# A cross-attention and RWKV-style layer in float32: the recurrence's four feature chunks are taken two at a time instead of one at a time

## The chip, the cores and the metric

The program runs on one core of one Trainium2 chip. The metric is the device time of one execution in microseconds (us). Four executions of the kernel before gave a median of 1838.74 us (1835.77 to 1843.25).

## The reference

The batch has 32 sequences of 128 tokens with 512 features, all in float32. Layer 0 is a cross attention over features, layer 1 an RWKV-style block whose core is a linear recurrence over the tokens.

```python
# layer 0, per sequence b (128 x 512)
A  = softmax((Wn @ inorm(x) + bn).T @ (Wm @ inorm(ctx) + bm))
x  = Wo @ ((Wl @ ctx + bl) @ A.T) + bo + x
# layer 1 (H = 32 heads of S = 16; its state comes from ctx)
xa = ln(x); sx = shift(xa)
xk, xw, xv, xr, xg = xa + sx * (maa + lowrank(xa + sx * maa_x))
w  = exp(-exp(time_decay + tanh(xw @ td_w1) @ td_w2))
r, k, v = xr @ Wr.T, xk @ Wk.T, xv @ Wv.T;  g = silu(xg @ Wg.T)
def step(s, r_t, k_t, v_t, w_t):              # per head, s is 16 x 16
    a   = outer(k_t, v_t)
    out = r_t @ (u * a + s)
    return a + w_t[:, None] * s, out
x1  = x + groupnorm(out) * g @ Wo.T
xc  = ln(x1); sx2 = shift(xc)
out = x1 + sigmoid((xc + sx2 * mr) @ Wfr.T) * (square(relu((xc + sx2 * mk) @ Wfk.T)) @ Wfv.T)
```

## The kernel before

**Tiling.** The 32 sequences are cut into `NG` = 8 groups of `G` = 4. A group's activations stand with features on the partitions: four feature chunks `c` of 128 features (8 heads) by `N` = 4 x 128 = 512 token columns. For each group the kernel runs `layer0` on its four sequences (stage "first"), and `layer1`: a "front" (norm, token shift, the five mixed inputs, the gates), the "recurrence" for each of the four chunks, and a "back" (group norm, the product with Wo, the feed-forward).

**The order is made by a planner.** No instruction is issued where the code names it. Every call goes to a recorder `K` (line 229 is where all recorded operations are emitted, so that nearly all the profile's rows say L229), and `schedule` then lists the operations of all engines in an order of its own: at each step it takes the operation that can start soonest by a table of costs, among equals the one with the lower rank, which is the place in the code less a little for what hangs on it. `with K.bunch(ns)` makes several matmuls one indivisible operation. Tiles come from pools with fixed numbers of slots: 54 work tiles `t` of 128 x 512, 8 PSUM `bank`s, two `rk`, two of each of the four `at`, two `vp`. An operation cannot be placed until its tile has a slot.

**The recurrence of one chunk** (`recurrence`, line 831) is a doubling scheme over the tokens. `r` and `k` lie side by side in one tile `rk`, `v` in a work tile; each comes from four accumulated matmuls (`proj`) and a ScalarE copy. Distances 1 and 2 are done by elementwise products on VectorE and a matmul with the block matrix `sum_bc` (banks `d0`, `d1`, `d2`). Then come four levels `l` = 4, 8, 16, 32, each of which is a handoff chain:

1. ScalarE makes `r2`, the right halves of `r` with even and odd heads masked apart (two `ACTIVATE t<-rk,par`).
2. TensorE multiplies `k` and `r2` in a bunch of 32 small matmuls on 32 x 64 tiles of the array into four banks `pa` (the bunch named 843 in the code).
3. VectorE copies the valid blocks from `pa` into the four `at` tiles (`COPY_PREDICATED`; at the last level ScalarE copies).
4. `twice(l)` multiplies the half blocks of `rk` in place by the running decays (`TENSOR_TENSOR rk<-rk,...`), which the next level reads.

After the levels `k` is transposed (`pk`, copied to `kt`), a bunch `ps` of 16 matmuls forms the state at the middle of the sequence, VectorE makes `s1` of it, and TensorE forms the outputs in two banks `po`: one bunch of 32 matmuls with the state, and two of 32 with `vp` and `at`. VectorE adds `po` to `acc`.

A matmul in float32 shows as two passes in the trace, so that a bunch of 32 matmuls is a line "x64". The array is used in different tile shapes: 128*128 for the large products, 32*64 for `pa`, 64*32 for `ps` and the `at` bunches, 32*32 for the `po` bunch with the state.

**What stands around it.** `layer1` calls `decays` for two chunks together and then `recurrence` for each chunk, and after each chunk records `layer0` for one sequence of the next group, which gives the planner other work to put between the handoffs. The feed-forward of the last but one group is recorded after the last group's recurrence.

Of the kernel before, what the change touches and what calls it, by code (L numbers as in the profile page):

```python
# [13 lines left out]
AF = mybir.ActivationFunctionType  # L14
# [18 lines left out]
T_SLOTS, SMALL_SLOTS, W_SLOTS = 54, 40, 4  # L33
Q4 = 4
EPS = 1e-5

# [503 lines left out]
def xattn_then_rwkv(ctx: ExitStack, tc: tile.TileContext, a: dict, out: bass.AP):  # L540
# [11 lines left out]
    rks = Pool(slots("rk", 2, [P, 2 * N]))  # L552
    weights = Pool(slots("wring", W_SLOTS, [P, NC * E]))
    ats = [Pool(slots(f"at{q}_", 2, [P, G * 2 * C])) for q in range(Q4)]
    vps = Pool(slots("vp", 2, [P, G * Q4 * 2 * DM]))
# [8 lines left out]
    def wt(shape=(P, 512)):  # L564
        return View(Tensor(work, list(shape)))

# [207 lines left out]
    def norm_shift(xs, w, bname, row, g):  # L774
        xns = []
        for x in xs:
            stats = st_(1, 6)
            K.vector.bn_stats(stats[:, 0, :], x)
            mv, rstd = mean_rstd(stats, 1)
            xn = wt()  # L780
            K.vector.tensor_scalar(
                xn, x, mv[:, 0, 0:1], rstd[:, 0:1], ALU.subtract, ALU.mult
            )
            xns.append(xn)
# [29 lines left out]
    def decays(c, dlow):  # L814

        pe = [bank() for _ in range(2)]
        with K.bunch(1050):
            for i in range(2):
                half = slice(i * DD, (i + 1) * DD)
                K.tensor.matmul(  # L820
                    pe[i], td2[half, (c + i) * P : (c + i + 1) * P], dlow[half], start=True, stop=True
                )
        got = []
        for i in range(2):
            ex = wt()
            K.scalar.activation(ex, pe[i], AF.Exp, bias=v_("time_decay", c + i))
            K.scalar.activation(ex, ex, AF.Exp, scale=-1.0)
            got.append(ex)
        return got

    def recurrence(c, ex, xk, xr, xv, wk, wr, s0m):

        rk = View(Tensor(rks, [P, 2, N]))
        r, k = rk[:, 0], rk[:, 1]
        K.scalar.copy(r, proj(wr, xr, c))
        K.scalar.copy(k, proj(wk, xk, c))
        v = wt()
        K.scalar.copy(v, proj(wv, xv, c))
# [4 lines left out]
        vp = View(Tensor(vps, [P, G * Q4 * 2 * DM]))  # L843
        at = [View(Tensor(p, [P, G * 2, C])) for p in ats]
        pt = bank()
        for b in range(G):
            K.tensor.transpose(pt[:, b * P : (b + 1) * P], v[:, b * P : (b + 1) * P], ident)
        K.scalar.copy(
            vp.view(0, (2 * DM, G * Q4), (DM + S, 2), (1, S)),
            pt.rearrange("p (x y j) -> p x y j", x=G * Q4, y=2),  # L850
        )


        x0, x1 = wt(), wt()
        K.vector.scalar_tensor_tensor(x0, k, v_("u", c), r, ALU.mult, ALU.mult)
        K.vector.tensor_tensor(x1[:, 0 : N // 2], r[:, 1::2], k[:, 0::2], ALU.mult)
        sums = sum_bc.rearrange("p h s -> p (h s)")
        d0, d1 = bank(), bank()
        K.tensor.matmul(d0, sums, x0, start=True, stop=True)
        K.tensor.matmul(d1[:, 0 : N // 2], sums, x1[:, 0 : N // 2], start=True, stop=True)  # L860
        acc = wt()

        def twice(h, tot):


            nb = N // (2 * h)
            s = rk.view(h, (N - h, 2), (2 * h, nb), (1, h))
# [8 lines left out]
        x2 = wt()  # L876
        K.vector.tensor_tensor(
            x2.view(0, (4, nb), (2, 2), (1, 2)),
            rk.view(2, (4, nb), (1, 2), (0, 2)),
            rk.view(N, (4, nb), (0, 2), (1, 2)), ALU.mult,  # L880
        )
        d2 = bank()
        K.tensor.matmul(d2, sums, x2, start=True, stop=True)
        tot = twice(2, tot)

        for li, l in enumerate(LEVELS):

            r2 = wt([P, G * 2, C])
            nb = C // (2 * l)
            for x in range(2):  # L890
                K.scalar.activation(
                    r2.view(x * (C // 2), (C, G * 2), (l, nb), (1, l)),
                    rk.view(l, (C, G * 2), (2 * l, nb), (1, l)),
# [3 lines left out]
            with K.bunch(843):  # L897
                for b in range(G):
                    for n in range(2):
                        for q in range(Q4):  # L900
                            rows_q = slice(q * DM, (q + 1) * DM)
                            K.tensor.matmul(
                                pa[q][n * C : (n + 1) * C, b * C : (b + 1) * C],
                                rk[rows_q, 1, b * L + n * C : b * L + (n + 1) * C],
                                r2[rows_q, 2 * b + n],
                                start=True, stop=True,
                            )
            for q in range(Q4):
                if l < C // 2:
                    K.vector.copy_predicated(  # L910
                        at[q].view(l, (C, 2 * G), (2 * l, nb), (1, l)),
                        level[l].view(0, (0, 2 * G), (l, nb), (1, l)),
                        pa[q].view(0, (C // 2, 2 * G), (l, nb), (1, l)),
                    )
                else:
                    for n in range(2):
                        sl = slice(n * C, n * C + l)
                        K.scalar.copy(
                            at[q][sl, :, l : 2 * l],
                            pa[q][sl, 0 : N // 2].rearrange("p (x t) -> p x t", t=l),  # L920
                        )
            tot = twice(l, tot)
            if li == 0:
                t1, t2 = wt(), wt()
                K.vector.tensor_tensor(acc, d0, v, ALU.mult)
                K.vector.tensor_tensor(
                    t1[:, 0 : N // 2], d1[:, 0 : N // 2], v[:, 0::2], ALU.mult
                )
                K.vector.tensor_tensor(acc[:, 1::2], acc[:, 1::2], t1[:, 0 : N // 2], ALU.add)
                nb = N // 4  # L930
                K.vector.tensor_tensor(
                    t2.view(0, (4, nb), (2, 2), (1, 2)),
                    d2.view(0, (4, nb), (2, 2), (1, 2)),
                    v.view(0, (4, nb), (0, 2), (1, 2)), ALU.mult,
                )
                right = acc.view(2, (4, nb), (1, 2))
                for s in range(2):
                    K.vector.tensor_tensor(right, right, t2.view(s, (4, nb), (2, 2)), ALU.add)


        s0t = wt([P, G, 2 * S])
        K.vector.tensor_tensor(
            s0t, s0m.view(c * 2 * S, (NC * 2 * S, G), (1, 2 * S)), tot.view(0, (2, G), (0, 2 * S)),
            ALU.mult,
        )
        pk = bank()
        for b in range(G):
            K.tensor.transpose(pk[0:C, b * P : (b + 1) * P], k[:, b * L : b * L + C], ident)
        kt = wt([C, N])
        K.scalar.copy(kt, pk[0:C, :])  # L950
        ps = bank()
        with K.bunch(385):
            for b in range(G):
                for q in range(Q4):
                    K.tensor.matmul(
                        ps[q * DM : (q + 1) * DM, b * DM : (b + 1) * DM],
                        kt[:, b * P + q * DM : b * P + (q + 1) * DM],
                        vp[0:C].view((b * Q4 + q) * 2 * DM, (DM + S, 2), (1, S)),
                        start=True, stop=True,
                    )  # L960
        s1 = wt([P, G, 2 * S])
        for x in range(2):
            of_x = (x * S, (2 * S, G), (1, S))
# [7 lines left out]
        with K.bunch(1020):  # L971
            for b in range(G):
                for n in range(2):
                    for q in range(Q4):
                        sl = slice(q * DM, (q + 1) * DM)
                        i = (b * NC + c) * DM
                        K.tensor.matmul(
                            po[n][sl, b * C : (b + 1) * C],
                            s1[sl, b, :] if n else s0m[sl, i : i + DM],
                            r[sl, b * L + n * C : b * L + (n + 1) * C],  # L980
                            start=(b == 0), stop=False, skip_group_check=True,
                        )
        for half in range(2):
            with K.bunch(720):
                for b in range(half * G // 2, (half + 1) * G // 2):
                    for x in range(2):
                        for n in range(2):
                            for q in range(Q4):
                                sl = slice(n * C, (n + 1) * C)
                                i = (b * Q4 + q) * 2 * DM + x * DM  # L990
                                K.tensor.matmul(
                                    po[n][q * DM : (q + 1) * DM, b * C : (b + 1) * C],
                                    vp[sl, i : i + DM], at[q][sl, 2 * b + x, :],
                                    start=False, stop=(x == 1), skip_group_check=True,
                                )
        for n in range(2):
            o = acc.view(n * C, (L, G), (1, C))
            K.vector.tensor_tensor(
                o, po[n][:, 0 : G * C].rearrange("p (b t) -> p b t", b=G), o, ALU.add
            )  # L1000
# [3 lines left out]
    def layer1(g, xs):  # L1004
        following = []
        K.stage = ("front", g)
# [108 lines left out]
        for c in range(NC):  # L1115
            K.stage = ("recurrence", g, c)
            if c % 2 == 0:
                ex = decays(c, dlow)
# [3 lines left out]
            o.append(recurrence(c, ex[c % 2], xm["k"], xm["r"], xm["v"], wk, wr, s0m))  # L1122
            if g + 1 < NG:
                following.append(layer0((g + 1) * G + c))
# [137 lines left out]
```

## Time and profile before

| | |
|---|---|
| median of four executions | 1838.74 us |
| the profiled execution, its own time | 1839.27 us |
| its span in the profile | 1837.5 us |
| busy: TensorE (PE), VectorE (DVE), ScalarE (ACT), GpSimd (POOL) | 1794.7, 1227.6, 751.3, 309.6 us |
| instructions: PE, DVE, ACT | 20264, 2754, 1501 |
| mean granted clock of TensorE | 0.996 |

Busy time of an engine is the time in which at least one of its instructions runs; the matmuls' ends are modelled and overlap, so start-to-start differences in the timeline are what a matmul costs its engine. "<-X" beside an idle time names the engine whose work ended it. PEld is TensorE's weight load.

### The profile page before, as it was taken

Reading aid. Unit: us, or ns where it says so; the run is one execution under the profiler, and the core shown is the slowest. Engines: PE = TensorE matmul, PEld = TensorE weight load, DVE = VectorE, ACT = ScalarE, POOL = GpSimd, SP = SyncE. Lnnn points to the kernel's source line nnn. Section 1 sums busy time; section 2 is a strip of 40 time slices with the busy share of each in tenths; the row PEclk is TensorE's granted clock in tenths of the full one; section 3 lists DMA queues with packets and bytes.
Section 4 is the critical chain, followed back from the end, with each engine's and each line's share of the span. In section 5 each row is a group of like instructions: output and inputs, shape, how many; then the busy total and the mean of one; then the engine's idle time right before and its main releaser. Section 6 shows DMA issues by size and latency. Waiting matters only on the chain.

```text
span 1837.5 us, 46377 instructions
## 1 busy us (share of the span) xinstructions
PE 1794.7 (98%) x20264; PEld 887.9 (48%) x20264; DVE 1227.6 (67%) x2754; ACT 751.3 (41%) x1501; POOL 309.6 (17%) x329
## 2 busy tenths in 40 slices
PE   8999999999999999999999999999999999999998
PEld 4345543555435554355543555435554455445543
DVE  8857883678746786467865678556784567866652
ACT  5345621546225462254522545225452355425421
POOL 2420014000150001500025000250002400240011
PEclk9999999999999999999999999999999999999999
DMA  7001102011110201102011110111201111001000
GB/s 230 1 25 45 54 23 92 25 62 37 46 69 25 73 26 46 69 33 66 25 52 63 40 63 21 52 63 40 71 13 58 58 40 48 2 24 48 26 18 29
DMA packets 61947, 87.29 MB, mean 48 GB/s; under 512 B 20336, under 2 KB 21488, under 8 KB 61744
## 3 DMA queue, kind: packets, MB, share of 16 engines
q1 hardware_dynamic: 61024, 84.06, 13.7%
q8 instruction: 159, 2.61, 0.6%
q14 instruction: 44, 0.36, 0.1%
q10 hardware_dynamic: 720, 0.26, 0.1%
HBM read 75.93 MB, written 8.39 MB: 46 GB/s over the span
## 4 chain that ended last, share of the span: by engine, by line
PE 89%; DVE 6%; ACT 2%; POOL 2%; issue 1%; POOLq 0%; DVEq 0%; ACTq 0%
PE bank L229 89%; DVE t L229 5%; ACT t L229 1%; POOL t L229 1%; DVE small L229 1%; ACT at L229 0%; POOL small L229 0%; DVE at L557 0%; DVE rk L229 0%; DVE at L229 0%; DVE vp L557 0%; POOLq L1258 0%; ACT L229 0%; ACT rk L229 0%; DVE fold L229 0%
## 5 line engine op out<-in xcount | busy, mean ns | idle before, releaser
L229 PE MATMUL bank<-t,wring 128*128 128x512 f32 x1024 | 488.5, 605 | 4.0 <-ACT t L229 2.1
L229 PE MATMUL bank<-wring,t 128*128 128x512 f32 x768 | 339.3, 599 | 8.6 <-DVE t L229 8.6
L229 POOL TENSOR_TENSOR t<-t,t 128x512 f32<-128x512 f32 x192 | 242.7, 1296 | 434.6 <-DVE t L229 422.0
L229 DVE TENSOR_TENSOR t<-bank,t 128x512 f32<-128x512 f32 (+1 forms) x256 | 147.6, 586 | 222.7 <-PE bank L229 191.8
L229 PEld LDWEIGHTS bank<-t,wring 128*128 128x128 f32 x1024 | 182.1, 190 | 221.3 <-issue 167.5
L229 PE MATMUL bank<-t,t 128*128 128x512 f32 x512 | 261.6, 614 | 0.7 <-ACT t L229 0.7
L229 POOL TENSOR_TENSOR small<-small,neg_half 128x1 f32<-128x1 f32 (+1 forms) x96 | 59.2, 631 | 1088.2 <-DVE small L229 1069.3
L229 PEld LDWEIGHTS bank<-wring,t 128*128 128x128 f32 x768 | 145.8, 192 | 196.8 <-issue 178.9
L229 ACT ACTIVATE t<-bank 128x512 f32<-128x512 f32 x120 | 71.8, 598 | 368.2 <-PE bank L229 368.0
L229 ACT COPY t<-bank 128x512 f32<-128x512 f32 (+1 forms) x240 | 135.1, 587 | 201.1 <-PE bank L229 199.8
L229 ACT ACTIVATE t<-rk,par 128x256 f32<-128x256 f32 x256 | 116.7, 501 | 129.4 <-DVE rk L229 115.7
L229 PE MATMUL bank<-ident,t 128*128 128x128 f32 x900 | 140.4, 278 | 6.8 <-DVE t L229 6.7
L229 ACT ACTIVATE t<-bank,small 128x512 f32<-128x512 f32 x128 | 87.9, 689 | 140.1 <-DVE small L229 139.6
L229 PEld LDWEIGHTS bank<-ident,t 128*128 128x128 f32 x900 | 104.3, 140 | 81.1 <-issue 46.3
L229 DVE COPY_PREDICATED at<-level,bank 128x256 f32<-128x256 int32 x384 | 143.2, 429 | 0.0
L229 DVE SCALAR_TENSOR_TENSOR t<-bank,vec,t 128x512 f32<-128x512 f32 x192 | 131.4, 743 | 16.2 <-PE bank L229 16.2
L229 PEld LDWEIGHTS bank<-t,rk 32*64 32x64 f32 x8192 | 99.8, 130 | 81.5 <-ACT t L229 53.2
L229 PE MATMUL bank<-t,wv 128*128 128x512 f32 x256 | 128.5, 601 | 0.0
L229 PEld LDWEIGHTS bank<-t,t 128*128 128x128 f32 x512 | 85.0, 191 | 77.5 <-issue 35.6
L229 PE MATMUL bank<-t,rk 32*64 32x64 f32 x8192 | 117.8, 230 | 1.7 <-issue 1.7
L229 DVE TENSOR_REDUCE small<-bank 128x1 f32<-128x512 f32 x128 | 88.0, 688 | 40.6 <-PE bank L229 40.2
L229 ACT COPY at<-bank 32x256 f32<-32x256 f32 x256 | 87.7, 361 | 24.0 <-PE bank L229 21.3
(94 smaller groups left out, 1884.4 us busy)
## 6 DMA issues: line engine op xcount, KB each, us to landing
t<-in_ctx_dram SPq DMA_DIRECT2D x32, 256.0 KB, 3.0
t<-in_x_dram SPq DMA_DIRECT2D x32, 256.0 KB, 2.7
wring<-in_WrT_dram SPq DMA_DIRECT2D x8, 1024.0 KB, 5.1
wring<-in_WkT_dram SPq DMA_DIRECT2D x8, 1024.0 KB, 5.0
wring<-in_WgT_dram SPq DMA_DIRECT2D x8, 1024.0 KB, 5.0
wring<-in_WoT_dram SPq DMA_DIRECT2D x8, 1024.0 KB, 5.3
out_dram<-t SPq DMA_DIRECT2D x32, 256.0 KB, 2.0
wring<-in_WfkT_dram SPq DMA_DIRECT2D x7, 1024.0 KB, 5.0
```

Of the source, the lines that this page charges most:

```text
L229: f(*[real(x) for x in args], **{k: real(x) for k, x in kw.items()})
```

## The change

Chunks 0 and 1, and chunks 2 and 3, go through the recurrence as one unit.

- `rk` is four rows of 512 (r, r, k, k) in two slots; `at` and `vp` are twice as wide, with one slot each instead of two. `decays` leaves both chunks' decays in one tile of a new pool `wide` (three slots of 128 x 1024), and `r2` comes from that pool too. The work pool has 44 slots instead of 54.
- Each VectorE and ScalarE operation of a level covers both chunks: `twice` 128 x 1024 instead of 128 x 512, the predicated copy 128 x 512 instead of 128 x 256, `r2` 128 x 512 instead of 128 x 256, the copies at the last level 32 x 512 instead of 32 x 256. `d1` of both chunks shares one bank and one matmul of 512 columns.
- Each bunch holds both chunks' matmuls: 64 instead of 32 in `pa` and in the `po` bunches, 32 instead of 16 in `ps`. The two halves of a chunk's `at` bunch become one bunch for each chunk. The transposes of `k` become a bunch of 8.
- `twice(l)` is recorded ahead of the predicated copies of its level; the part that fills `acc` from `d0`, `d1`, `d2` ahead of the levels.
- `layer0` of the next group's sequences is recorded at other places: sequence 0 ahead of the first pair's recurrence, 1 after it, 2 after the second pair's, and 3 after the product with Wo.
- The arguments `after`, `HOLD` and `LATE` are new, and at the values set here (0 and 2) leave the feed-forwards where they were.

```diff
-T_SLOTS, SMALL_SLOTS, W_SLOTS = 54, 40, 4
+T_SLOTS, SMALL_SLOTS, W_SLOTS, WIDE_SLOTS = 44, 40, 4, 3
+AHEAD, AHEAD_B = ((1,), (2,), (), (3,)), ((0,), ())
+HOLD, LATE = 0, 2
...
-    rks = Pool(slots("rk", 2, [P, 2 * N]))
+    rks = Pool(slots("rk", 2, [P, 4 * N]))
+    wides = Pool(slots("wide", WIDE_SLOTS, [P, 2 * N]))
-    ats = [Pool(slots(f"at{q}_", 2, [P, G * 2 * C])) for q in range(Q4)]
-    vps = Pool(slots("vp", 2, [P, G * Q4 * 2 * DM]))
+    ats = [Pool(slots(f"at{q}_", 1, [P, 2 * G * 2 * C])) for q in range(Q4)]
+    vps = Pool(slots("vp", 1, [P, 2 * G * Q4 * 2 * DM]))
...
         def twice(h, tot):
-            nb = N // (2 * h)
-            s = rk.view(h, (N - h, 2), (2 * h, nb), (1, h))
+            nb = N // h
+            s = rk.view(h, (2 * N - h, 2), (2 * h, nb), (1, h))
             K.vector.tensor_tensor(s, s, tot.view(0, (1, 2), (2, nb), (0, h)), ALU.mult)
...
-            with K.bunch(843):
-                for b in range(G):
-                    for n in range(2):
+            with K.bunch(2 * 843):
+                for i in range(2):
+                    for b in range(G):
+                        for n in range(2):
...
+            tot = twice(l, tot)
             for q in range(Q4):
                 if l < C // 2:
                     K.vector.copy_predicated(
-                        at[q].view(l, (C, 2 * G), (2 * l, nb), (1, l)),
+                        at[q].view(l, (C, 4 * G), (2 * l, nb), (1, l)),
...
-            tot = twice(l, tot)
-        pk = bank()
-        for b in range(G):
-            K.tensor.transpose(pk[0:C, b * P : (b + 1) * P], k[:, b * L : b * L + C], ident)
+        pk = [bank() for _ in range(2)]
+        with K.bunch(875):
+            for i in range(2):
+                for b in range(G):
+                    K.tensor.transpose(
+                        pk[i][0:C, b * P : (b + 1) * P], k[i][:, b * L : b * L + C], ident
+                    )
...
-        with K.bunch(385):
+        with K.bunch(2 * 385):
...
-        with K.bunch(1020):
+        with K.bunch(2 * 1020):
...
-        for half in range(2):
-            with K.bunch(720):
+        for i in range(2):
+            with K.bunch(2 * 760):
...
-        for c in range(NC):
-            if c % 2 == 0:
-                ex = decays(c, dlow)
-            o.append(recurrence(c, ex[c % 2], xm["k"], xm["r"], xm["v"], wk, wr, s0m))
-            if g + 1 < NG:
-                following.append(layer0((g + 1) * G + c))
+        for c in range(0, NC, 2):
+            ex = decays(c, dlow)
+            ahead(*AHEAD_B[c // 2])
+            o += recurrence(c, ex, xm["k"], xm["r"], xm["v"], wk, wr, s0m)
+            ahead(*AHEAD[c // 2])
```

## The prediction

> **What bounds the kernel now.** I read the page first: busy times, the clock, the chain that ended last.
>
> ```profile
> PE 1794.7 (98%) x20264; PEld 887.9 (48%) x20264; DVE 1227.6 (67%) x2754; ACT 751.3 (41%) x1501; POOL 309.6 (17%) x329
> PEclk9999999999999999999999999999999999999999
> PE 89%; DVE 6%; ACT 2%; POOL 2%; issue 1%; POOLq 0%; DVEq 0%; ACTq 0%
> ```
>
> TensorE is the bound: at full clock throughout, 98% busy, 89% of the chain. So time can come only from what its stream costs, and from its waits. The view of waits, PE alone, names these:
>
> ```profile
> PE bank L229 <- DVE t L229: 18.9, 20, 2.3
> PE bank L588 <- DMA WoT<-in_WoT_dram: 6.1, 1, 6.1
> PE bank L229 <- ACT t L229: 5.3, 10, 1.8
> PE bank L229 <- POOL t L229: 3.2, 12, 0.4
> ```
>
> All PE idle time sums to 37.5 us. By the timeline: start 7.3; group 0's front 5.0; six sets of 0.86 in the fronts; six pairs around the feed-forward's norm (0.81 and 1.00 below), 11.1; the last two groups 9.0, of it 3.8 in the turn from group 6 to 7.
>
> ```profile
> 456.73 0.66 PE L229 MATMUL bank<-ident,t 128*128 128x128 f32 x4 [0.81 <-DVE t L229]
> 463.28 14.00 PE L229 MATMUL bank<-wring,t 128*128 128x512 f32 x32 [1.00 <-DVE t L229]
> ```
>
> Then the timeline of PE inside a recurrence, for the price of a bunch.
>
> ```profile
> 334.11 0.91 PE L229 MATMUL bank<-t,rk 32*64 32x64 f32 x64
> 334.95 1.13 PE L229 MATMUL bank<-t,wv 128*128 128x512 f32 x2
> 335.91 1.02 PE L229 MATMUL bank<-t,wring 128*128 128x512 f32 x2
> 336.77 1.02 PE L229 MATMUL bank<-t,wv 128*128 128x512 f32 x2
> 337.72 0.91 PE L229 MATMUL bank<-t,rk 32*64 32x64 f32 x64
> 338.57 0.66 PE L229 MATMUL bank<-ident,t 128*128 128x128 f32 x4
> ```
>
> Read start to start. A large product between large products takes 0.86 (335.91 to 336.77). Ahead of a bunch it takes 0.95 (to 337.72): 0.09 to go in. The first one after a bunch takes 0.96 (334.95 to 335.91): 0.10 more, as its second pass comes late. The bunch takes 0.85. What two bunches save by standing together, six places of this trace show:
>
> ```profile
> 158.31 0.86 PE L229 MATMUL bank<-at,vp 64*32 64x64 f32 x64
> 159.10 1.13 PE L229 MATMUL bank<-t,wring 128*128 128x512 f32 x2
> 427.03 1.48 PE L229 MATMUL bank<-at,vp 64*32 64x64 f32 x128
> 428.44 1.98 PE L229 MATMUL bank<-t,t 128*128 128x512 f32 x4
> ```
>
> One takes 0.79, two joined 1.41: 0.17 less than twice 0.79.
>
> **The change, part by part.** I counted the tile shapes along PE's instruction order in the built programs, before and after.
>
> *Fewer changes of shape.* The matmuls are the same but for `d1` (two of 256 columns become one of 512, the same columns: nothing). Runs in the 32*64 shape go from 128 to 62, in 64*32 from 90 to 48, in 32*32 from 32 to 16: 124 fewer. Runs of the other shapes grow by 7. The transposes of `k` pay nothing at their edges (0.11 each, inside or at the end). One merge saves 0.17 + 0.09 + 0.10 = 0.36 where a large product follows, 0.26 where a transpose does. I take 0.33: 124 x 0.33 = 41, less 7 x 0.28 = 2 for the new runs: **39 us off PE's stream**, bounds 30 and 43. Only the 64*32 shape was seen joined; the others are costed by it.
>
> *Waits that go.* In the new order, between the last product with Wo and the last eight transposes of the feed-forward's norm stand 3.7 us of other PE work (sequence 0 of the group after next, the next front's transposes), and 3.4 us before its first product; before, 1.7 us stood at the first place. The last sequence's norm needs 3.5 there (0.25 from PE to DVE, add 0.69, statistics 0.69 + 0.17 + 0.15, POOL's power 0.59, scaling 0.56, handoffs 0.4). So the six pairs vanish: **-11.1**, bounds -11.1 and 0. Next there come the fronts' 0.86 waits, which I keep.
>
> *Longer handoffs.* The other engines' rows:
>
> ```profile
> L229 DVE TENSOR_TENSOR rk<-rk,t 128x512 f32<-128x512 f32 x96 | 66.4, 691 | 45.8 <-PE bank L229 40.3 <-issue 3.3
> L229 DVE COPY_PREDICATED at<-level,bank 128x256 f32<-128x256 int32 x384 | 143.2, 429 | 0.0
> L229 ACT ACTIVATE t<-rk,par 128x256 f32<-128x256 f32 x256 | 116.7, 501 | 129.4 <-DVE rk L229 115.7 <-DVE small L229 8.4 <-issue 5.2
> ```
>
> DVE loses 452 instructions at about 0.15 of fixed cost each (256 columns 0.42, 512 columns 0.69), ACT 217. Neither bounds the kernel, so this is worth nothing by itself; but each handoff is now longer. Doubled: the decay product 0.69 + 0.54 = 1.23; an `r2` 0.50 + 0.22 = 0.72, the second starting 0.42 + 0.22 = 0.64 after the first; a predicated copy about 0.70. In the trace DVE starts 0.25 after the bunch's last matmul, ACT 0.04 after DVE, PE 0.06 after its releaser, and PE is free 0.15 after the last matmul. From one `pa` bunch to the next of its chain a pair needs 0.25 + 1.23 + 0.04 + 0.64 + 0.72 + 0.06 - 0.15 = 2.8 us of other PE work; one chunk needs 1.9. From the last `pa` to the transposes of `k`: 1.4. From `ps` to the first `po` bunch: 0.8.
>
> What stands between in the new order, in groups 1 to 5: for the first pair 5.2, 3.4 and 4.3 us between the levels, nothing before the transposes of `k`, 0.9 before `ps`; for the second pair 4.6, 3.4, 3.4, then 1.5, 1.5 and 0.7. So the first pair waits 1.4 at the transposes; about 0.7 at `ps`, where ACT makes five copies of the last level (0.5 each) before the two of `kt`; and about 1.0 at the levels, because between two of its decay products DVE has some 8 us of other rows (the other pair's distances, `acc`, four predicated copies) for 7 us of PE work. The second pair waits about 0.5. That is 3.6 a group, six groups: **+21.6**; bounds 0 (the 3 to 5 us of cover hold everywhere, and the transposes' wait falls into slack that I did not see) and 33 (1.9 more a group at the levels, one late DVE row each). I take the middle, as the orders name the places.
>
> *The last two groups*, where no `layer0` is left. In group 6's second pair 0.2 us stand between the third and fourth `pa`, none before `ps` and `po`: 2.6 + 1.5 + 0.8 = 4.9. In group 7's second pair three `pa` bunches stand side by side: 2 x 2.8 = 5.6. Against this go 0.8 and 3.7 of waits there before; add 0.5 at the turn, whose two chains have less between them: **+6.5**, bounds 3 and 10.
>
> *Instruction supply.* The page's queue of 159 instruction packets (2.61 MB) is PE's: 16 KB a packet, 64 bytes for each of its 40528 matmuls and loads, so 256 a packet. The closest two packets start 3.36 us apart. Now a bunch of 64 is 256 instructions in some 1.6 us. It has run dry once, in dense bunches of the last group:
>
> ```profile
> 1704.28 0.81 PE L229 MATMUL bank<-t,rk 32*64 32x64 f32 x53
> 1706.45 0.36 PE L229 MATMUL bank<-t,rk 32*64 32x64 f32 x11 [1.36 <-issue]
> ```
>
> The densest 13.6 us of the new order hold 1270 instructions, before 930; at 256 per 3.36 us plus two packets in hand that is 1540, so it should last: **+2**, bounds 0 and 8.
>
> *Nothing.* The single slots of `at` and `vp` bind the second pair's first predicated copy to the first pair's last `po` bunch; in the new order that copy's `pa` comes 1.4 us behind it. SP issues the same transfers; those of `layer0` keep their holds, and DMA engines are 10 to 20% busy with landings of 3 us against recurrences of 60; uncovered, one late load would cost 3. Wo and the feed-forward's weights still wait for an operation between the pairs; they land in 5 us and are used 40 us later. Table loads are 44 against 45.
>
> **Sum**: -39 - 11.1 + 21.6 + 6.5 + 2 = -20 us. From the profiled execution's own 1839.27 (span 1837.5 and 1.8 around it) this gives **1819 us**; the median of the runs is 0.5 lower, which I neglect. The waits would stand at 37.5 - 11.1 + 21.6 + 6.5 + 2 = 56.5.
>
> One rule speaks against longer waits. In the row above the clock is full in all 40 slices, with waits up to 2.3 us. The Trainium skill, "TensorE: Matmul & The Clock Gate", section "Why this matters for your kernels", warns of idle gaps over about 3 us, after which the clock falls to half; no row here shows it past the start. By it the three waits of 2.6 to 2.8 us just escape; if they tipped over, an estimate from the window of 3.4 us in that page's Part 1 is 1.7 us lost for each, and the sum would be 1824.
>
> **The rivals.**
> - *The whole gain arrives*: the handoffs stay covered in groups 0 to 5. For it: the order before had single handoffs with 1.9 to 2.1 us of cover against 1.9, and its trace shows no wait there. Against: at the transposes of `k` nothing at all stands between. -39 - 11.1 + 6.5 = 1796 us. 0.23.
> - *VectorE sets the pace at the levels* (slower). It does whole pairs between two `pa` bunches, and with 8 us of rows in 7 us every level of every pair comes late: 16 pairs x 3 handoffs x 1.2 us = 58, less the 6 counted: 1819 + 52 = 1871. It decides once all waits pass 37.5 + 39 = 76.5. Against it: DVE's mean load is 67% and falls. With the instruction supply as the same kind of loss, 0.12.
> - *Nothing comes of it*: the waits grow by what the stream loses, 1834 to 1844. 0.11.
> - That the change doesn't do what it says is excluded by the counted order.
>
> **How the numbers follow.** A measurement of this kernel can tell about 0.3%, 5.5 us, from no change. The forecast, 1805 to 1833, has 0.54; its own range is that of the handoffs' bounds. With the whole gain (1785 to 1805) faster has 0.77; same 0.11; slower 0.12. Leaving about a tenth out on each side gives 1793 to 1842.
>
> **What would show it.** The waits of PE rise to some 55 us while PE's busy time falls to about 1756; the 32*64 bunches appear as x128 and take some 1.5 us start to start; the waits before the feed-forward's norm are gone; a wait on DVE `rk` appears before the transposes of `k` once a group. It would be wrong if PE's busy time fell by less than 30, if the waits passed 75, or if they stayed below 40 (the whole gain).

## The result: no change, 1840.72 us against 1839.22

The changed kernel takes 1840.72 us (median of 34 executions, 1834.47 to 1847.60), the kernel before beside it 1839.22 (56 executions). The ratio is 1.0007, 95% interval 1.0000 to 1.0013. A second measurement of both on another occasion (`after_ref` below) gave 1.0030, 1.0017 to 1.0042; so figures of different occasions may stand 0.2% apart, and kernels are compared below where they ran together. The forecast was 1819. The profiled execution took 1841.98, its span 1840.3 (before 1837.5).

The page of the changed kernel, in the lines that were read of the kernel before: busy times, clock, chain.

```profile
PE 1775.8 (96%) x20232; PEld 888.3 (48%) x20232; DVE 1169.9 (64%) x2301; ACT 701.5 (38%) x1228; POOL 308.5 (17%) x329
PEclk9999999999999999999999999999999999899899
PE 86%; DVE 8%; ACT 4%; issue 1%; DMA 0%; POOL 0%; ACTq 0%; POOLq 0%; DVEq 0%
```

VectorE lost 57.7 us and ScalarE 49.8, as the doubled operations had to give; neither is the bound. TensorE's busy time fell by 18.9 us, not by 39. In the last sixth of the span the clock row shows an 8 twice. The waits of PE, with total, number and longest:

```profile
PE bank L231 <- DVE t L231: 12.6, 11, 3.0
PE bank L231 <- issue: 10.6, 16, 2.9
PE bank L231 <- ACT wide L231: 9.0, 3, 3.4
PE bank L231 <- DVE rk L231: 7.3, 5, 1.5
```

All PE idle time is 58.9 us against 37.8 (the prediction has 37.5); the forecast was 56.5. `DVE rk` (before the transposes of `k`) and `ACT wide` (before a `pa` bunch) are longer handoffs of the recurrence; `issue`, where nothing that the profile shows was waited for, rose from 1.7 to 10.6. The timeline of PE at the end of the first pair of group 1 shows what a handoff now costs:

```profile
387.57 1.59 PE L231 MATMUL bank<-wide,rk 32*64 32x64 f32 x128
390.63 1.06 PE L231 MATMUL bank<-ident,rk 128*64 128x128 f32 x8 [1.47 <-DVE rk L231]
...
393.12 0.76 PE L231 MATMUL bank<-vp,t 64*32 64x32 f32 x64 [0.57 <-ACT t L231]
...
453.52 1.12 PE L231 MATMUL bank<-t,WmT 128*128 128x512 f32 x2 [1.11 <-DVE t L231]
```

The 1.47 before the transposes of `k` and the 0.57 before `ps` (forecast 1.4 and 0.7) come in each of groups 1 to 5. The wait in the last line is in the feed-forward region. The forecast had that pair of waits (1.81 a group) gone; 1.11 of it stays.

The same stretches of both kernels, last pair of group 6 and of group 7, in the view by windows (length, PE busy and its instructions, the other engines; the granted clock follows after POOL). First the kernel before, then the changed one:

```profile
1560.00:1600.00 40.00, 37.80 (x612) 19.34 (x610) 32.19 (x66) 20.95 (x40) 5.58 (x6) 1.00 0.01 2
1716.00:1740.00 24.00, 23.11 (x560) 12.88 (x564) 18.57 (x43) 13.45 (x30) 0.00 (x0) 1.00 0.01 4
```

```profile
1560.00:1600.00 40.00, 30.55 (x722) 17.73 (x714) 27.98 (x48) 15.45 (x24) 10.36 (x9) 0.85 0.01 2
1716.00:1740.00 24.00, 20.15 (x604) 12.84 (x605) 16.63 (x30) 8.81 (x16) 0.00 (x0) 0.79 0.01 3
```

A mean of 0.79 over 24 us is 10 us at half clock. The clock records of the whole span have 13.7 us at half clock before (four stretches of 3.41 us) and 37.5 after (11 of them). TensorE is busy in 13.4 us of these before and in 34.3 after, and half of that is lost: 6.7 against 17.2. The other executions agree: the mean clock was 0.985 to 0.992 in those of the changed kernel, 0.995 to 1.000 in those of the kernel before.

So the span splits as follows, PE's starts taken one from the next and the waits left out:

| | before | after | difference | forecast |
|---|---|---|---|---|
| PE's stream, as if at full clock throughout | 1787.4 | 1758.1 | -29.3 | -39 |
| lost to half clock | 6.7 | 17.2 | +10.5 | 0 |
| waits | 37.8 | 58.9 | +21.2 | +19 |
| rest (the tail) | | | +0.4 | 0 |
| span | 1837.5 | 1840.3 | +2.8 | -20 |

Of the 22.8 us between forecast and result the clock makes 10.5, the stream 9.7, the waits 2.2 and the tail 0.4.

### The profile page after: what moved, and what is told of

It is laid out like the page before. It is cut to its first block, busy times and chain, and to the rows that moved or that the text cites. A ratio compares the mean times of both kernels' runs of the same rounds, so it can differ in the third digit from the quotient of the medians.

```text
span 1840.3 us, 45443 instructions
## 1 busy us (share of the span) xinstructions
PE 1775.8 (96%) x20232; PEld 888.3 (48%) x20232; DVE 1169.9 (64%) x2301; ACT 701.5 (38%) x1228; POOL 308.5 (17%) x329
## 4 chain that ended last, share of the span: by engine, by line
PE 86%; DVE 8%; ACT 4%; issue 1%; DMA 0%; POOL 0%; ACTq 0%; POOLq 0%; DVEq 0%
PE bank L231 86%; DVE t L231 3%; ACT at L231 2%; DVE at L231 2%; ACT t L231 2%; DVE small L231 1%; DVE rk L231 1%; DMA WoT<-in_WoT_dram 0%; ACT wide L231 0%; ACTq L586 0%; POOLq L1300 0%; ACT L231 0%; POOL t L231 0%; PE bank L594 0%; POOL small L231 0%
## 5 line engine op out<-in xcount | busy, mean ns | idle before, releaser
L231 PE MATMUL bank<-t,wring 128*128 128x512 f32 x1024 | 474.3, 602 | 0.6 <-DVE t L231 0.6
L231 PE MATMUL bank<-wring,t 128*128 128x512 f32 x768 | 344.0, 600 | 0.0
L231 PEld LDWEIGHTS bank<-t,wring 128*128 128x128 f32 x1024 | 186.5, 191 | 241.8 <-issue 213.1
L231 PE MATMUL bank<-t,t 128*128 128x512 f32 x512 | 255.5, 607 | 0.9 <-ACT t L231 0.8
L231 ACT ACTIVATE wide<-rk,par 128x512 f32<-128x512 f32 x128 | 85.4, 714 | 123.5 <-DVE rk L231 123.5
L231 PEld LDWEIGHTS bank<-wide,rk 32*64 32x64 f32 x8192 | 96.4, 133 | 58.3 <-issue 29.0
L231 DVE COPY_PREDICATED at<-level,bank 128x512 f32<-128x512 int32 x192 | 124.4, 710 | 0.0
L231 PE MATMUL bank<-t,wv 128*128 128x512 f32 x256 | 123.7, 599 | 0.2
L231 PE MATMUL bank<-wide,rk 32*64 32x64 f32 x8192 | 106.9, 235 | 14.8 <-ACT wide L231 9.0
L231 DVE TENSOR_SCALAR t<-t,small,small 128x512 f32<-128x512 f32 x128 | 68.8, 553 | 35.2 <-POOL small L231 34.9
```

What stands on the lines that cost most here:

```text
L231: f(*[real(x) for x in args], **{k: real(x) for k, x in kw.items()})
```

## Experiments

**Theory A**, from this table: the gain was smaller than costed (a run of one shape that goes saves about 0.25, not 0.33), and the half clock and the supply of instructions are costs of their own, which the denser bunches and the waits beside them bring. **Theory B**: the stream's gain is there in full, but it is only the planner's other order, or the handoffs, that eat it; take the waits away and the time follows them.

### What a break in a bunch costs: e_head, e_mid

Every `pa` bunch of the changed kernel gets one transpose of 128 columns more, in `e_head` ahead of its matmuls, in `e_mid` between the two chunks; the order is otherwise that of the changed kernel. The extra work is the same, and only `e_mid` breaks the bunch.

```diff
# e_head, ahead of "for i in range(2)"; e_mid has the same in that loop, under "if i:"
+                K.tensor.transpose(pa[0][:, N // 2 : N // 2 + P], ident, ident)
+                K.bunch_op.words -= 2
```

> The changed kernel with one extra 128-column transpose ahead of the first matmul of each of its 64 joined pa bunches; the order of all else is the same. Where the transpose stands it has the shape of the work before it, so no change of shape is added. Both theories: 64 x 0.11 = 7 us more busy time of PE than the changed kernel (1775.8 to about 1783).

> The same transpose in the middle of each joined pa bunch, so that 32*64 runs go from 62 to 126 while the order and all handoffs stay. Theory A (a break in a bunch has the price that I read from the trace before, 0.26 to 0.36 us, and the loss lies elsewhere): 64 x 0.25 = 16 us more than the run with the transpose at the head. Theory B (joining gains little on this chip): under 5 us more.

Measured together: `e_head` 1848.03, `e_mid` 1868.84 us (ratios to before 1.0037, 1.0025 to 1.0049, and 1.0149, 1.0130 to 1.0169). The pages' first rows, `e_head` and then `e_mid`:

```profile
PE 1783.2 (97%) x20296; PEld 897.9 (49%) x20296; DVE 1170.4 (63%) x2301; ACT 702.3 (38%) x1228; POOL 307.9 (17%) x329
```

```profile
PE 1808.7 (97%) x20296; PEld 908.1 (49%) x20296; DVE 1172.9 (63%) x2301; ACT 702.9 (38%) x1228; POOL 307.1 (16%) x329
```

A break costs 20.8 / 64 = 0.33 us of time. The two spans are 19.8 us apart: reckoned at full clock, PE's stream grew by 15.7, 0.25 for each break; 9.9 us more were lost to half clock (the work in it rose from 35.7 to 55.5), and the waits were 6 us less. So joining does save time. At 0.25 for each of the 124 runs, less 2 for the seven new ones, it would be 29, near the measured 29.3; but that is not yet the reason. The break here is made by a transpose, for which the prediction itself has 0.26; its 0.36, where a large product follows, is not tested by any run. What else slowed the joined bunches stands under "Why the prediction was wrong".

### One part alone, on the kernel before: b_at, b_l0

`b_at` joins the two halves of a chunk's `at` bunch; `b_l0` records the last sequence's `layer0` after the product with Wo.

```diff
# b_at
-        for half in range(2):
-            with K.bunch(720):
-                for b in range(half * G // 2, (half + 1) * G // 2):
+        for half in range(1):
+            with K.bunch(1440):
+                for b in range(G):
# b_l0
-            if g + 1 < NG:
+            if g + 1 < NG and c < NC - 1:
...
+        if g + 1 < NG:
+            following.append(layer0((g + 1) * G + NC - 1))
+            K.stage = ("back", g)
```

> The kernel before, with the two at bunches of each chunk joined into one of 64; nothing else of the change. 26 joins fewer runs in 64*32. Theory A: 26 x 0.33 = 9 us less busy time of PE, and about that in the time, as no handoff grows. Theory B: nothing (within 3 us).

> The kernel before, with the layer0 of the next group's last sequence recorded after the product with Wo; nothing else of the change. If that placement fills the waits around the feed-forward's norm: about 11 us of waits less, 1828. If the waits only move: within 4 us of before.

Both missed: 1864.88 (1.0137, 1.0116 to 1.0158) and 1883.59 (1.0236, 1.0216 to 1.0256). The planner ordered the whole program anew: in `b_at` the 64*32 runs fell from 90 to 64 as meant, but all runs only from 737 to 729. Their waits of PE, `b_at` and then `b_l0`:

```profile
PE bank L229 <- DVE small L229: 21.3, 7, 3.5
```

```profile
PE bank L229 <- DVE small L229: 20.2, 6, 3.6
PE bank L229 <- DVE t L229: 20.1, 24, 2.4
```

The new wait of 3.5 us a group stands before the group norm's product (`heads_t`), for which nothing else was left to do. In `b_at` one or two stretches at half clock follow each of these six waits; of the 24 us that its span grew, 10.9 are waits and 12.8 are lost to half clock. Both runs test the edit together with a new plan; of the price of a shape they say nothing. What they show is that the places of the other work are worth more than the change itself.

### The placement of layer0: a_l0

The changed kernel with `layer0` of the four sequences recorded after the recurrences of the two pairs, two each.

```diff
-AHEAD, AHEAD_B = ((1,), (2,), (), (3,)), ((0,), ())
+AHEAD, AHEAD_B = ((0, 1), (2, 3), (), ()), ((), ())
```

> The changed kernel with layer0 of the next group recorded where the kernel before had it (two sequences after each pair, none ahead of a recurrence or after the product with Wo). If the new placement is what filled the waits around the feed-forward's norm: about 1.9 us a group come back, 11 us in all, 1852. If the pairs' own handoffs decide: within 4 us of 1841.

Measured 1855.92 (1.0080, 1.0064 to 1.0096), 1852 expected. The waits on `DVE t` rose from 12.6 to 19.6 us, now in 28 places, and PE's busy time to 1787.1. So with the old places the changed kernel loses to the kernel before. The order was planned anew here too, so how much of this is the places themselves isn't shown; in `b_l0` a new place alone made the kernel before slower.

### Filling the waits: e_keep

Twenty-one products of 128 x 512 that nobody needs are put into the waits of the last two groups: three before each later `pa` bunch of the second pairs, three after group 6's reciprocal.

```diff
...
+            for j in range(3 if last_two and prev is not None else 0):
+                K.held = prev
+                K.tensor.matmul(pa[j], wv[:, 0, 0:P], wv[:, 1, :], start=True, stop=True)
...
+        for j in range(3 if g == NG - 2 else 0):
+            K.held = heads_op
+            K.tensor.matmul(pb[j], wv[:, 0, 0:P], wv[:, 1, :], start=True, stop=True)
```

> The changed kernel with 21 extra large products (128x512, of weights, their results overwritten): three ahead of each of the second to fourth pa bunch of the second pair in groups 6 and 7, held until the bunch before has been issued, and three ahead of the product that follows group 6's reciprocal. They fill PE waits with array work and shorten no handoff. Theory A (after a window with a mostly empty array the clock is halved, which costs the changed kernel some 11 us more than the kernel before): the half-clock time there (20 us of windows) goes, granted clock from 0.989 to about 0.995, and although work is added the time falls by 5 to 10 us, to about 1833. Rival (the waits alone cost, the clock does not): 1841 or up to 5 us more.

Measured 1847.85 (1.0034, 1.0021 to 1.0047): no gain. Nine of the products stood where no wait was; PE's busy time rose by 15.7 to 1791.5, the waits fell by 9.8 to 49.1, the work at half clock from 34.3 to 23.0. Added work and removed losses came out about even. `issue` stands at 14.4 us in 26 places; two more profiles of the changed kernel itself have 11.5 in 21 and 11.9 in 23, so that filled waits are followed by a late supply is not shown. As a test of the clock alone it was badly built, and the next one is better.

### The same, only where the wait is: after_ref, e_keep7

`after_ref` is the changed kernel as it is; `e_keep7` has six products, three in each of the two long waits of group 7's second pair. They ran together.

```diff
...
+            for j in range(3 if K.stage[1] == NG - 1 and c == 2 and l >= 16 else 0):
+                K.held = prev
+                K.tensor.matmul(pa[j], wv[:, 0, 0:P], wv[:, 1, :], start=True, stop=True)
```

> The changed kernel again, timed on the same chip as the next three, as their reference: 1840 to 1846.

> The changed kernel with six extra large products (5.2 us of array work, results overwritten) in the two exposed waits of group 7's second pair (3.4 and 3.0 us between the pa bunches), three in each; nothing else is added. Theory A (the half clock costs by itself): the waits there become busy time, the 10.2 us of half-clock windows behind them go, and the time is about 4 us below the changed kernel on the same chip, though 5.2 us of work are added. Rival (only waits cost): no change, within 1.5 us.

Measured 1845.30 (1.0030, 1.0017 to 1.0042) and 1842.74 (1.0007, 0.9997 to 1.0017). The timelines of PE there, the changed kernel and then `e_keep7`:

```profile
1716.86 1.88 PE L231 MATMUL bank<-wide,rk 32*64 32x64 f32 x128 [3.38 <-ACT wide L231]
1721.73 2.25 PE L231 MATMUL bank<-wide,rk 32*64 32x64 f32 x128 [2.99 <-ACT wide L231]
```

```profile
1720.16 1.60 PE L231 MATMUL bank<-wide,rk 32*64 32x64 f32 x128 [0.60 <-ACT wide L231]
1721.69 2.84 PE L231 MATMUL bank<-wv 128*128 128x512 f32 x6
1725.03 1.59 PE L231 MATMUL bank<-wide,rk 32*64 32x64 f32 x128 [0.50 <-ACT wide L231]
```

And the view by windows of `e_keep7` there, with the clock at 1.00 instead of 0.79:

```profile
1716.00:1740.00 24.00, 22.80 (x690) 13.51 (x674) 19.76 (x36) 9.85 (x17) 0.00 (x0) 1.00 0.02 3
```

With the waits filled by useless work the bunch takes 1.59 instead of 2.25, the 10.2 us at half clock there are gone, and the kernel is 2.6 us faster although PE does 5.2 us more. That is less than the 4 us expected, and by the spread of the twelve runs of each the gain lies between 1.2 and 6.0. The half clock is a cost of its own at this place; theory B, by which the time follows the waits alone, falls here.

### Which half-clock stretches and stalls recur: after_again, e_hold

`after_again` is the changed kernel once more. `e_hold` keeps the last group's three feed-forward weights from being loaded until the first pair is done, because a stall of 2.91 us on `issue` at 1669.88 fell beside these loads.

```diff
# e_hold, in layer1's loop over the pairs and at the weights
+            if c == 0:
+                first_done = K.ops[-1]
...
-            ws = [weight(n, third) for n in ("Wfk", "Wfr", "Wfv")]
+            ws = [weight(n, third if g < NG - 1 else first_done) for n in ("Wfk", "Wfr", "Wfv")]
```

> The changed kernel once more, for a second profile. Waits of PE as in the first (58.9 us within 3). If the half-clock windows depend on where a free-running window falls over the low stretches, the windows in groups 1 to 5 differ from the first profile's three, while those of the last two groups, with waits of about 3 us, come again.

> The changed kernel with the last group's three feed-forward weight loads held until the first pair's recurrence is done (the order on PE is the same), so that they no longer run beside the dense bunches at 1663 to 1670 us. Theory A (the wait of 2.9 us inside a pa bunch there is PE's instruction packet held up by these loads): it falls below 0.6 and the half-clock window behind it goes, some 4 us less in all. Rival (the bunches are too dense for the supply by themselves): the wait stays at 2 to 3 us.

`after_again` took 1845.61, with the same waits (`issue` 11.9, `DVE t` 12.8, `ACT wide` 8.8, `DVE rk` 7.3). Its half-clock stretches in the last two groups are again there (1570 to 1608, and 10.2 us from 1720). Of the earlier ones most stand at the 1.11 us wait in the feed-forward region, once a group, and which groups have one differs: from 676.7 and 1127.3 in the first profile, from 454.2, 679.4, 1130.0 and 1358.7 here. `e_hold` took 1845.68 (1.0030, 1.0019 to 1.0040), like the changed kernel. Its stall at that place is 0.86 us, but `after_again` has 0.83 there without the edit, so the length of that one stall was chance. Whether weight loads lengthen such a stall at all stays open.

### Another place for the last feed-forward: a_late3, late3_keep7

`a_late3` records two feed-forwards after the last recurrence instead of one; `late3_keep7` adds the six products.

```diff
-HOLD, LATE = 0, 2
+HOLD, LATE = 0, 3
```

> The changed kernel with LATE set to 3: group 5's feed-forward is recorded after group 6's recurrence and group 6's after group 7's, so that group 6's tail has other work. In its order no handoff of group 6's second pair stands uncovered. If the waits of 2.6, 2.1, 0.9 and 3.0 us there and the half-clock windows behind them (13.7 us at half rate) are what the pairs lost: some 8 us of waits and 6 of clock less, 12 us in all, about 1831. If they only move: within 4 us of the changed kernel.

> Both: group 6's tail filled by the feed-forward of group 5, and the six extra products in group 7. By theory A the two gains add: about 16 us below the changed kernel, 1827, faster than the kernel before.

`a_late3` missed by far: 1867.16 (1.0152, 1.0134 to 1.0170). All groups were ordered anew; the largest of PE's waits, against 12.6 us in 11 places:

```profile
PE bank L231 <- DVE t L231: 22.7, 29, 4.3
```

`late3_keep7` took 1863.35 (1.0129, 1.0112 to 1.0145), far from the 1827 expected, but 3.8 us less than `a_late3` with 5 us more work: the second time that filling these two waits pays.

### Spacing the bunches out: a_words

The planner has its own table of TensorE's supply: words in hand, and a refill's time. Here it is told 4.8 us for a refill.

```diff
-WORDS, REFILL = 280, 3200
+WORDS, REFILL = 280, 4800
```

> The planner of the kernel after is told that a refill of TensorE's queue takes 4.8 us instead of 3.2, and so puts dense bunches farther apart; the whole order is planned anew, with 458 runs of one shape against 463. If the supply's stalls are a cost by themselves, the waits on issue fall from 10.6 us to under 5 and the time to about 1836. If they stand in for handoff waits that would otherwise be there, or the new order brings other waits, the sum of PE's waits stays at 55 to 75 us and the time is 1840 to 1860. I take the second for the likelier.

1883.90 (1.0226, 1.0209 to 1.0243): worse than either theory. `issue` rose to 19.4 us and `DVE t` to 28.8. A new plan again; the stalls can't be planned away by this number.

### Supply and clock by themselves: m_probe, m_probe2

Behind the last operation of the changed kernel, PE runs pieces of extra work whose results nobody reads.

```diff
     with tc.manual_schedule():
         K.run()
+        probe()     # large(n): n products 128x512; narrow(): one joined pa bunch;
+                    # wait(b, n): VectorE copies bank b n times
```

> Behind the whole work of the kernel after, TensorE does extra work whose results nobody reads; stretches of 16 large products (24 before the first) part the pieces. Piece 1: 12 joined `pa` bunches without a break. Piece 2: 10 times (bunch, 4 large products). Piece 3: 10 times (bunch, 2 large). Piece 4: 12 times (2 large, then a wait for two VectorE copies). Piece 5: 12 times (bunch, the same wait). Piece 6: 12 times (1 large, a wait for four copies). Supply, theory A (a packet of 256 instructions takes about 3.3 us to come, and less than two are in hand): piece 1 takes 12 x 3.3 = 40 us less at most one packet, with one stall of 1 to 2 us for each bunch from the second or third on; piece 2 has no stall (5.1 us each); piece 3 stands at the limit, 3.3 to 3.4 us each. Theory B (two packets in hand, and packets come as fast as they are asked for): piece 1 takes 12 x 1.5 = 18 us and nothing stalls. Clock, theory A (a narrow bunch counts little, so that short waits beside it are enough): half-clock stretches in piece 5 with its waits of some 1.3 us, and none in piece 4 with the same waits; in piece 6 (some 2.5 us of waiting for 0.9 of work) they come too. Theory B (only a wait of about 3 us or more counts): none in pieces 4, 5 and 6.

> Extra work on TensorE behind that of the kernel after, as in the first probe, with 16 large products between the pieces, each 12 times. Piece 1: 1 large product, a wait of 1.5 us. Piece 2: 4 large, 3.0. Piece 3: 4 large, 4.4. Piece 4: a joined bunch, 1 large, 1.5. Piece 5: bunch, 3 large, 1.5. Piece 6: bunch, 6 large, 3.0. Theory A (what counts is the work in a stretch of 3.41 us, a large product in full and a narrow bunch by an eighth; below 0.25 to 0.4 the next stretch is at half clock): piece 1 with 0.36 stands at the edge; in pieces 2 and 3 stretches that hold nearly nothing but the wait are followed by half clock, now and then in piece 2 and more often in piece 3; piece 4 (0.27) is at half clock throughout; piece 5 (0.5 in the mean, 0.2 where a bunch and a wait fall together) shows some; piece 6 shows it after nearly every wait. Theory B (a wait must pass about 3.4 us by itself, and narrow work counts as work): half clock in piece 3 alone.

*Supply.* The timeline of `m_probe`, piece 1 (bunches without a break; one bunch is x128) and piece 2 (bunch, 4 large products):

```profile
1853.28 2.53 PE L1273 MATMUL bank<-wide,rk 32*64 32x64 f32 x215
1858.09 2.11 PE L1273 MATMUL bank<-wide,rk 32*64 32x64 f32 x128 [2.28 <-issue]
1861.84 2.25 PE L1273 MATMUL bank<-wide,rk 32*64 32x64 f32 x128 [1.64 <-issue]
...
1911.46 1.59 PE L1273 MATMUL bank<-wide,rk 32*64 32x64 f32 x128
1912.98 3.70 PE L1264 MATMUL bank<-wv 128*128 128x512 f32 x8
```

After 20 us of large products the queue gave 215 matmuls with their loads, 430 instructions, and then stalled. The next came 4.8 us after the beginning, and from there 256 per stall, every 3.66 us in the mean ((1894.72 - 1858.09) / 10). Each stall ends 1.2 to 1.6 us after an instruction packet landed. Piece 2 (272 instructions in 5.16 us) never stalls; piece 3 (264 in 3.4) falls back to 3.76 us a turn, at full clock, with two short stalls and bunches of up to 1.98 instead of 1.59. Theory A of the expectation holds in kind; a packet takes 3.66 us where it has 3.3.

*Clock.* The view by windows again, inside pieces 4 (2 large products, wait) and 5 (bunch, wait) of `m_probe`:

```profile
2030.00:2068.00 38.00, 21.82 (x44) 7.45 (x44) 14.82 (x22) 0.00 (x0) 0.00 (x0) 1.00 0.00 0
2087.00:2125.00 38.00, 22.83 (x1303) 20.77 (x1300) 13.83 (x20) 0.00 (x0) 0.00 (x0) 0.55 0.02 4
```

And pieces 1 (1 large, short wait), 2 (4 large, long wait) and 4 (bunch, 1 large, short wait) of `m_probe2`:

```profile
1862.00:1900.00 38.00, 21.62 (x22) 5.05 (x21) 15.05 (x22) 0.00 (x0) 0.00 (x0) 0.53 0.00 0
1920.00:2003.00 83.00, 49.84 (x89) 19.28 (x88) 30.98 (x45) 0.00 (x0) 0.00 (x0) 0.88 0.00 0
...
2158.00:2206.00 48.00, 31.27 (x1430) 20.20 (x1430) 15.35 (x23) 0.00 (x0) 0.00 (x0) 0.93 0.01 4
```

All nine pieces with waits, by the same view:

| beside each wait | wait, us | granted clock |
|---|---|---|
| 2 large products | 1.51 | 1.00 |
| 1 large product | 1.51 | 0.53 |
| one joined bunch | 1.51 | 0.55 |
| one joined bunch and 1 large | 1.51 | 0.93 |
| one joined bunch and 3 large | 1.51 | 1.00 |
| 1 large | 2.96 | 0.50 |
| 4 large | 2.96 | 0.88 |
| one joined bunch and 6 large | 2.96 | 0.80 |
| 4 large | 4.41 | 0.72 |

The same wait of 1.51 us costs nothing beside two large products and half the clock beside one: the wait's length alone doesn't decide, but how much work stands in the few microseconds around it. That is theory A in kind. Its figure for a bunch (an eighth of a large product's weight) is wrong: a bunch and one large product stayed at full clock but for one place, and with three large ones throughout, where half clock was expected now and then. Beside the 2.96 us waits the loss comes even after six large products. In piece 1 of `m_probe`, bunches with stalls of 1.2 to 2.3 us between them also ran at half clock throughout, so that a lack of instructions brings the clock down as a handoff does.

## Why the prediction was wrong

**The clock, 0.** This is the step that failed outright: it was weighed and dismissed, with "the three waits of 2.6 to 2.8 us just escape". It cost +10.5 us; even the 5 us named there for the case that these waits tip over are half of that. The forecast took a threshold on the length of a wait for the whole condition. The kernel before spoke against that: "at full clock throughout" is not so. Its clock records have four stretches at half clock, at waits of 1.94, 1.05 and 2.29 us and, from 1707.8, after the stall of 1.36 that the prediction shows. Two of them in the view by windows:

```profile
1366.42:1369.83 3.41, 3.41 (x5) 1.35 (x4) 3.41 (x7) 0.00 (x0) 0.00 (x0) 0.50 0.00 0
1707.75:1711.16 3.41, 3.41 (x12) 0.87 (x19) 1.90 (x6) 1.88 (x4) 0.00 (x0) 0.50 0.00 0
```

The slice row hid them, since a slice is 46 us long and 3.41 us at half clock leave its mean at 0.96. The Trainium skill, "TensorE: Matmul & The Clock Gate", section "Why this matters for your kernels", warns of idle gaps over about 3 us. The runs here differ: half clock came with waits of 1.51 us beside one bunch or one large product, and in the changed kernel at 676.7, behind the 1.11 us wait before the feed-forward. Here the measurement decides.

**The instruction supply, +2.** Its stalls rose by 8.9 us. The rate assumed (256 per 3.36, and two packets in hand, 1540 in 13.6 us) was too good. With the probe's numbers, 430 in hand, the next after 4.8 us and 256 every 3.66, some 1198 come in 13.6 us; the densest stretch of the new order holds 1270. The closest two packets of a trace in which the supply is hardly ever short are no measure of its steady rate, nor do they tell what is in hand.

**The stream, -39.** The count of runs was right; the stream fell by 29.3, just short of the lower bound given. The costing took every joined bunch as undisturbed, and many were not. The joined `pa` bunches did take the 1.5 us of the forecast where nothing held them up; joined `at` bunches, 1.41 in five of the six places of before, took 1.535 in the median, and only 11 of 32 took 1.41. In 18 of the other 21 the longest pause between two matmuls, 0.07 to 1.05 us, ends 2.2 to 2.9 us after an instruction packet began, as the stalls of `m_probe` do (2.25 to 2.99): the supply again, in pauses mostly too short to count as waits. Over all joined bunches at full clock the time above that of an undisturbed one of the same kind sums to 7.9 us; in the bunches of the kernel before it is 1.9. So some 6 of the missing 9.7 us are such slower starts; the rest stays open.

**The waits.** In total right, 58.9 against 56.5, and by luck, since the terms were off both ways. The waits in the fronts, which the forecast kept (5.2 us, and 5.0 in group 0), are gone. The longer handoffs of groups 0 to 5 came to 14.9 instead of 21.6: they stand where they were named, 1.47 and 0.57 in each of groups 1 to 5, but there are none at the levels, for which 1.0 a group was allowed. The feed-forward's waits, which were to vanish, stand at 7.2, since 1.11 of 1.81 a group stayed. Those of the last two groups came to 17.2 without the stalls, some 3 more than the forecast (2.6 and 2.1 in group 6, 3.4 and 3.0 in group 7, 2.95 at the turn). And 8.9 of the rise is the supply.

**The rivals.** VectorE did not set the pace at the levels, and the whole gain did not arrive. "Nothing comes of it", given 0.11, is what happened, but only in part by its reason: the stream lost 29.3, the waits gained 21.2 and the half clock 10.5. Of the signs named beforehand, "PE's busy time fell by less than 30" was the one that came true. One count was off without touching the sum: ScalarE lost 273 instructions, not 217.

What stays open is how the planner's reorderings cost what they do: `b_at`, `b_l0`, `a_late3` and `a_words` changed a line or two each and lost 20 to 45 us, in waits that no one placed there and, where it was reckoned (`b_at`), as much in the half clock behind them. No version here beats the kernel before.

## What to carry to other kernels

Price joined bunches of small matmuls from a break in a bunch at full clock (here 0.25 us, the break being a transpose), and set their instructions against the queue's steady supply (here 256 per 3.66 us) before counting a gain: work made denser than that returns as stalls. A wait on TensorE has a second price, the clock: read the clock records, not the row of 40 slices, and ask what stands beside a wait, not only how long it is; two large products beside a wait of 1.5 us were enough. Where a planner orders everything, count the waits of the new order place by place, since a one-line edit there moved more time than the change itself.

## What the runs showed of the hardware

- Half-clock stretches are multiples of 3.41 us, and which of the shorter waits brings one differs between executions of one program; those at the long waits of the last two groups came in each of three profiles of the changed kernel.
- Alone between waits, a bunch of 64 small matmuls shows 1.59 us at full and 2.27 at half clock, a large product 1.13 and 2.07.
- TensorE's instructions came in packets of 256, at a steady 3.66 us each when the queue was drained, with 430 in hand after a rest; a stall ended 1.2 to 1.6 us after its packet had landed.
- Useless work of 5 us in two waits made the kernel 2.6 us faster.
